# A selective scan that takes two channel tiles in one instruction

## The chip, the cores and the metric

The kernel runs on one core of a Trainium2 chip. The metric is the device time of one execution in microseconds, taken as the median of several runs. The core has a matrix engine (TensorE, PE in the profile; PEld is its weight load), VectorE (DVE), ScalarE (ACT), GpSimd (POOL) and SyncE (SP), which here issues nearly all DMA transfers. Each engine works through its own instructions in order.

## The reference, cut to what matters

One decoder layer in float32 on x of shape (8, 512, 512): a Mamba block, cross-attention with 16 heads, and a mixture of 32 experts with a shared expert, each followed by a residual sum and a layer norm. The change touches the Mamba block:

```python
xz = layernorm(x) @ in_proj_w                    # (b, s, 2048): x_main, z
x_main = silu(causal_conv(x_main, 4 taps))       # 1024 channels
dt, B, C = split(x_main @ x_proj_w)              # 32, 16, 16 wide
dt = softplus(dt @ dt_proj_w + dt_proj_b)        # (b, s, 1024)
h[t] = exp(A * dt[t]) * h[t-1] + dt[t] * B[t] * x_main[t]   # 1024 channels x 16 states
y[t] = sum over states of h[t] * C[t]
out = ((y + x_main * D) * silu(z)) @ out_proj_w + x
```

It also moves two buffers of the experts' routing: softmax over 32 experts, the best 4 of 8 groups, the best 4 experts, and their slots.

## The kernel before, in words

The program has three parts in sequence: `layers` (Mamba, attention, routing and shared expert of all 8 batches), `experts` (the 32 experts) and `finish` (last layer norm). The change is in `layers`.

*Tiles of the scan.* Channels lie on partitions: 1024 channels are 8 tiles of 128, taken as four pairs `q`. Time is cut into two chunks of 256 steps a batch, so there are 16 chunks. The 16 states are taken in groups of four. For one channel tile and one group the kernel keeps a state tile `h` of 128 partitions x 4 rows x 257 columns. Column 0 of each row holds the state carried from the chunk before; the other 256 hold dt·B·x, and after the scan the states. The partitions hold two halves of 64 channels with different states, which is why dt and dt·x are first copied by DMA into tiles `both` in that arrangement.

*One step.* A step is one (pair q, group g, tile ci of the pair); a chunk has 32, numbered k. Each step runs these functions:

- `carry` (L443, ScalarE) takes a state tile `h` from a ring of four and writes column 0 from `l_state`, or zeros from `l_nothing` in a batch's first chunk.
- `decays` (L437, ScalarE) writes exp(A·dt) of the *next* step into one of two tiles `l_da`, four activations of 256.
- `scan` (VectorE) writes the product dt·x·B into `h` (L449), runs the recurrence over all 4 x 257 columns in one scan instruction (L453; column 0 of `l_da` is zero, so rows do not mix), and in the first chunk of a batch stores the last column in `l_state` (L455).
- `collect` multiplies `h` by C (L470, VectorE) and sums over states on PE into the PSUM tile `py` (L474; at the first group also the D·x term, L462).

At the end of a pair `gated` multiplies `py` into the gate `zs` (L486).

*What else is in a chunk.* `prepare` (L392 on PE, then L402 to L418 on ScalarE and VectorE, then the DMA copies into `both`, L426) makes the next pair's dt and dt·x with softplus written as relu and logarithm. `bcast` (L381) copies rows of B and C to all partitions, tiles `bc`. Around fixed steps k stand the output projection of the chunk before (`back`, L503), the gate projection (`gate_x`, L305), and for the next chunk the layer norm, the input projection (L305), the convolution (`convolve`, VectorE taps at L339, buffer `xp`) and `x_proj` (L362). Between them the attention, the shared expert and the routing of the batch before are spread as "side" work by a running sum of costs: scores (L766), their row maxima on VectorE (`mx`, L768), exponentials (`eT`, L796), weighted sums (L808), dense products (L703), and the routing chain (`choose`, L546 to L602; `locate` after it).

*Order.* `do` holds back the later parts of a piece of work to the next call (`settle`), and the scheduler that builds the program fixes each engine's final order, so instructions of neighbouring steps are mixed. Pools with a fixed number of buffers decide how far a step can run ahead: `h` has four, `bc` four, `l_da` two, `both` two, and `u`, `dt`, `l`, `dtx`, `xp` one each.

Of the kernel before, what the change touches and what calls it, by code (L numbers as in the profile page):

```python
# [16 lines left out]
P = 128  # L17
B, S, D = 8, 512, 512
# [4 lines left out]
DI = 1024  # L23
NST = 16
RANK = 32
# [56 lines left out]
def layers(ctx, tc, a, x1d, filld, based, xbuf):  # L82
# [76 lines left out]
    nothing = cp.tile([P, NG, 1], F32, name="l_nothing")  # L159
    nc.gpsimd.memset(nothing, 0.0)  # L160
    das = [cp.tile([P, NG, T + 1], F32, name=f"l_da{i}") for i in range(2)]
    for da in das:
        nc.gpsimd.memset(da[:, :, 0:1], 0.0)

# [23 lines left out]
        channel_multiplier=0,  # L188
    )

    early = cp.tile([P, SC, E], F32, name="l_early")
    nc.gpsimd.iota(
        early, pattern=[[0, SC], [-1, E]], base=E, channel_multiplier=0, allow_small_or_imprecise_dtypes=True
    )
    first = cp.tile([P, SC, E], F32, name="l_first")
    nc.gpsimd.iota(
        first, pattern=[[0, SC], [CAP, E]], base=-SLOTS, channel_multiplier=0, allow_small_or_imprecise_dtypes=True
    )

    taken = cp.tile([P, SC + 1, E], F32, name="l_taken")  # L200
    nc.gpsimd.memset(taken, 0.0)
# [67 lines left out]

    piece = pieces()  # L270

    def load_x(b, t, f):
        f["xt"] = xt = p1.tile([P, NT_, D], F32, tag="xt", name="xt")
        nc.sync.dma_start(xt, a["x"][b, t * T : (t + 1) * T, :].rearrange("(j p) d -> p j d", p=P))
# [39 lines left out]
    def convolve(t, q, f):  # L314

        c0 = 2 * q
        ps = project(f, "ps_x")

        def first_tap():
            xp = p1.tile([P, 2, T + 3], F32, tag="xp", name="xp")  # L320
            if t == 0:
                nc.gpsimd.memset(xp[:, :, 0:3], 0.0)
            else:
                nc.gpsimd.tensor_copy(xp[:, :, 0:3], conv_tail[:, c0 : c0 + 2, :])
            nc.scalar.copy(xp[:, :, 3:], ps)
            if t < S // T - 1:
                nc.gpsimd.tensor_copy(conv_tail[:, c0 : c0 + 2, :], xp[:, :, T : T + 3])
            f["xs"][q] = xs = p2.tile([P, 2, T], F32, tag="xs", name="xs", bufs=6)
# [13 lines left out]

            return other_taps

        return first_tap
# [28 lines left out]
    def bcast(f, g):  # L374

        got = []
        for r0 in (g * NG, NST + g * NG):
            t = bcp.tile([P, NG // 2, T], F32, tag="bc", name="bc")
            for r in range(2):
                n0 = r0 + r * NG // 2  # L380
                nc.sync.dma_start(  # L381
                    t[r * HP : (r + 1) * HP], f["scr"][n0 : n0 + NG // 2, :].partition_broadcast(HP)
                )
            got.append(t.unsqueeze(1).to_broadcast([P, 2, NG // 2, T]))
        return got

    def prepare(q, f):

        ps = psm.tile([P, 2, T], F32, tag="mm", name="ps_dt")
        for i in range(2):  # L390
            c = 2 * q + i
            nc.tensor.matmul(  # L392
                ps[:, i, :], w_dt[:, c * P : (c + 1) * P], f["xd"][0:RANK, :], start=True, stop=True
            )

        def exponentials():
            u = p1.tile([P, 2, T], F32, tag="u", name="u")
            dt = p1.tile([P, 2, T], F32, tag="dt", name="dt")

            for i in range(2):  # L400
                c = 2 * q + i
                nc.scalar.activation(u[:, i, :], ps[:, i, :], AF.Abs, bias=b_dt[:, c : c + 1])  # L402
                nc.scalar.activation(dt[:, i, :], ps[:, i, :], AF.Relu, bias=b_dt[:, c : c + 1])
            nc.scalar.activation(u, u, AF.Exp, scale=-1.0)
            l = p1.tile([P, 2, T], F32, tag="l", name="l")
            nc.scalar.activation(l, u, AF.Ln, bias=1.0)
            w = dtx = p1.tile([P, 2, T], F32, tag="dtx", name="dtx")
            nc.scalar.activation(w, u, AF.Identity, bias=1.0)

            def both():  # L410

                nc.vector.scalar_tensor_tensor(w, w, -1.0, u, ALU.add, ALU.subtract)
                nc.vector.tensor_tensor(l, l, w, ALU.subtract)
# [19 lines left out]
    def decays(c, g, dt, da):  # L433

        for n in range(NG):
            j, m = n // 2, n % 2
            nc.scalar.activation(da[:, n, 1:], dt[:, c % 2, j, :], AF.Exp, scale=aneg[:, c, j, g, m : m + 1])  # L437

    def carry(t, c, g):

        last = state[:, c, g].unsqueeze(2)
        h = p3.tile([P, NG, T + 1], F32, tag="h", name="h", bufs=4)
        nc.scalar.copy(h[:, :, 0:1], last if t else nothing)  # L443
        return h

    def scan(t, c, g, dtx, bc, da, h):

        steps = h.rearrange("p (j m) t -> p j m t", j=2)[:, :, :, 1:]
        nc.vector.tensor_tensor(  # L449
            steps, dtx[:, c % 2].unsqueeze(2).to_broadcast([P, 2, NG // 2, T]), bc[0], ALU.mult  # L450
        )
        flat = h.rearrange("p n t -> p (n t)")
        nc.vector.tensor_tensor_scan(flat, da.rearrange("p n t -> p (n t)"), flat, 0.0, ALU.mult, ALU.add)  # L453
        if t < S // T - 1:
            nc.vector.tensor_copy(state[:, c, g].unsqueeze(2), h[:, :, T : T + 1])  # L455

    def collect(c, g, h, bc, py, f):


        if g == 0:  # L460
            for j in range(2):
# [8 lines left out]
        nc.vector.tensor_tensor(steps, steps, bc[1], ALU.mult)  # L470
        for m in range(NG // 2):
            for j in range(2):
                s = (g, m, c % 2)
# [70 lines left out]
    def choose(b, x2t, pl, st):  # L544
# [16 lines left out]
        eq = gm.tile(square, F32, tag="g_eq", name="g_eq")  # L561
        nc.vector.tensor_tensor(eq, other, own, ALU.is_equal)
        nc.vector.tensor_tensor(eq, eq, lower.unsqueeze(1).to_broadcast(square), ALU.mult)
        gt = gm.tile(square, F32, tag="g_gt", name="g_gt")
# [458 lines left out]
    for i, (b, t) in enumerate(chunks):  # L1023
# [8 lines left out]
        for k, (q, g, ci) in enumerate(steps):  # L1032
            if ci == 0:
                if (q, g) != (CC // 2 - 1, NST // NG - 1):
                    bcn = bcast(f, (g + 1) % (NST // NG))
                else:
                    bcn = bcast(nf, 0) if after else None
            h = carry(t, 2 * q + ci, g)

            if k + 1 < len(steps) or after:  # L1040
                nq, ng, ni = steps[(k + 1) % len(steps)]
                decays(2 * nq + ni, ng, (f if k + 1 < len(steps) else nf)["ready", nq][0], das[(n + 1) % 2])
            scan(t, 2 * q + ci, g, f["ready", q][1], bc, das[n % 2], h)
            n += 1
            if k % 8 == 0:
                if k:
                    gated(q - 1, f, py)
# [371 lines left out]
```

## Time and profile before

| | |
|---|---|
| median of 3 runs | 5617.29 us (5615.69 to 5618.11) |
| the profiled execution | 5620.06 us, its span 5617.3 us |
| busy PE / PEld / DVE / ACT / POOL | 4888.6 / 2725.6 / 4351.5 / 2592.2 / 546.1 us |
| scan L453: count, mean | 512, 2295 ns |
| product with B, L449 | 512, 1216 ns |
| product with C, L470 | 512, 1220 ns |
| exponentials L437 | 2048, 499 ns |
| scan stage, first scan to last | 84 to 3730 us of the span |

A row of the groups of instructions reads: line, engine, operation, output from inputs, shapes, count, then busy time and the mean of one in ns, then the idle time of the engine just before these instructions and what ended it. A row of the waits reads: who waited at which line for whom, the time in all, how often, the longest. A row of the timeline reads: start and duration in us, engine, line, operation, with the idle time before it in brackets.

### The profile page before, as it was taken

The numbers are of one execution on the slowest core, as the hardware profiler recorded it, in microseconds if no ns is written. First come the engines' busy times: TensorE is split into PE (matmuls) and PEld (weight loads), VectorE is DVE, ScalarE is ACT, GpSimd is POOL, SyncE is SP. The second block draws the span as 40 slices with busy tenths as digits, with TensorE's granted clock in tenths as the row PEclk, the third lists the DMA queues.
The fourth block names the chain that finished last, engine by engine and source line by source line (L and its number), as shares of the span: only waits on it lengthen the run. The fifth ranks groups of instructions, "written<-read, shape, count | busy, mean of one in ns | idle before, by whom it ended". The sixth has DMA issues, their size and how long they took to land. (4 is left out here: it accounts for less than half of the span.)

```text
span 5617.3 us, 60406 instructions
## 1 busy us (share of the span) xinstructions
PE 4888.6 (87%) x19752; PEld 2725.6 (49%) x19752; DVE 4351.5 (77%) x5738; ACT 2592.2 (46%) x5480; POOL 546.1 (10%) x424
## 2 busy tenths in 40 slices
PE   5667888888888988888888898879899999999994
PEld 3333344434433434443443443333577777777773
DVE  5988888989889998898989899854555655555554
ACT  4454555655556555565545656523122222222223
POOL 0000002001100200200010020010111111111111
PEclk8778999999999999999999999989899999999997
DMA  6777345434534534543463453431444444444444
GB/s 207 215 219 201 99 129 177 128 112 130 189 107 113 190 107 122 177 132 106 124 204 94 125 183 110 115 118 45 137 124 126 124 124 119 125 126 124 120 117 138
DMA packets 560426, 769.83 MB, mean 137 GB/s; under 512 B 135754, under 2 KB 268394, under 8 KB 560112
## 3 DMA queue, kind: packets, MB, share of 16 engines
q1 hardware_dynamic: 522608, 680.70, 40.2%
q0 software_dynamic: 33280, 76.90, 7.0%
q10 hardware_dynamic: 4224, 8.39, 0.4%
q8 instruction: 156, 2.56, 0.2%
q14 instruction: 158, 1.29, 0.1%
HBM read 508.68 MB, written 165.05 MB: 120 GB/s over the span
## 5 line engine op out<-in xcount | busy, mean ns | idle before, releaser
L437 ACT ACTIVATE l_da<-both,l_aneg 128x256 f32<-128x256 f32 x2048 | 888.4, 499 | 801.8 <-DVE h L453 759.7
L453 DVE TENSOR_TENSOR_SCAN h<-l_da,h 128x1028 f32<-128x1028 f32 x512 | 1171.2, 2295 | 48.5 <-ACT h L443 26.4
L474 PE MATMUL py<-h,l_twice 128*64 128x256 f32 x4096 | 628.1, 420 | 217.4 <-DVE h L470 217.3
L449 DVE TENSOR_TENSOR h<-both,bc 128x1024 f32<-128x1024 f32 x512 | 619.2, 1216 | 97.2 <-PE py L474 45.4
L470 DVE TENSOR_TENSOR h<-h,bc 128x1024 f32<-128x1024 f32 x512 | 623.5, 1220 | 6.0
L474 PEld LDWEIGHTS py<-h,l_twice 128*64 128x64 f32 x4096 | 295.3, 147 | 587.6 <-DVE h L470 260.7
L766 PE MATMUL ps_s<-l_ka,l_qa 64*128 64x512 f32 x1024 | 317.1, 699 | 142.9 <-DVE mx L768 142.7
L1199 PE MATMUL ps_h<-xT,w 128*128 128x320 f32 x1536 | 435.6, 433 | 0.0
L1279 POOL DMA_INDIRECT based<-y,xe x160 | 250.5, 1565 | 1317.2 <-ACT y L1302 579.9
L768 DVE TENSOR_REDUCE mx<-ps_s 128x2 f32<-128x1024 f32 x256 | 310.8, 1217 | 83.7 <-PE ps_s L766 82.9
L1220 DVE TENSOR_TENSOR hT<-ps_h,p 128x320 f32<-128x320 f32 x128 | 62.9, 492 | 374.7 <-PE ps_h L1199 374.6
L1199 PEld LDWEIGHTS ps_h<-xT,w 128*128 128x128 f32 x1536 | 292.4, 191 | 118.4 <-issue 0.8
L792 PE MATMUL ps_t<-l_qa,l_ka 64*128 64x512 f32 x1024 | 302.0, 654 | 15.8 <-ACT eT L796 11.9
L796 ACT ACTIVATE eT<-ps_t 128x1024 f32<-128x1024 f32 x256 | 259.1, 1013 | 111.9 <-PE ps_t L792 111.5
L808 PE MATMUL po<-eT,l_va 128*64 128x512 f32 x1024 | 279.2, 623 | 23.0 <-ACT raw L820 19.0
L1199 PE MATMUL ps_h<-t,s 128*128 128x320 f32 x1024 | 286.1, 432 | 0.0
L641 POOL DMA_INDIRECT xbuf<-x2t,dest x128 | 216.7, 1693 | 622.1 <-DVE dest L635 583.7
L305 PE MATMUL ps_z<-xnT,wm 128*128 128x256 f32 x1024 | 246.3, 395 | 31.2 <-DMA wm<-in_in_proj_w 28.4
L503 PE MATMUL po<-wm,zs 128*128 128x512 f32 x512 | 246.7, 634 | 13.0 <-DMA wm<-in_out_proj_w 8.5
L703 PE MATMUL ps_p<-x2T,wa 128*128 128x512 f32 x512 | 244.7, 627 | 11.1 <-DVE hT L883 9.1
L305 PE MATMUL ps_x<-xnT,wm 128*128 128x256 f32 x1024 | 245.3, 393 | 1.4 <-ACT xnT L294 1.1
L305 PEld LDWEIGHTS ps_z<-xnT,wm 128*128 128x128 f32 x1024 | 196.2, 196 | 83.7 <-ACT l_da L437 27.1
(225 smaller groups left out, 7397.0 us busy)
## 6 DMA issues: line engine op xcount, KB each, us to landing
bc<-scr SPq DMA_DIRECT2D x1024, 128.0 KB
w<-in_w SPq DMA_DIRECT2D x96, 1024.0 KB
wm<-in_in_proj_w SPq DMA_DIRECT2D x128, 512.0 KB
xbuf<-zero SPq DMA_DIRECT2D x32, 1362.5 KB
xe<-xbuf SPq DMA_DIRECT2D x32, 1362.5 KB
both<-dt SPq DMA_DIRECT2D x256, 128.0 KB
both<-dtx SPq DMA_DIRECT2D x256, 128.0 KB
wm<-in_out_proj_w SPq DMA_DIRECT2D x64, 512.0 KB
```

The costliest lines, as they stand in the source:

```text
L305: nc.tensor.matmul(ps[:, i, :], w[:, dc, i * P : (i + 1) * P], f["xnT"][:, dc, :], start=(dc == 0), stop=(dc == DC - 1),)
L437: nc.scalar.activation(da[:, n, 1:], dt[:, c % 2, j, :], AF.Exp, scale=aneg[:, c, j, g, m : m + 1])
L449: nc.vector.tensor_tensor(steps, dtx[:, c % 2].unsqueeze(2).to_broadcast([P, 2, NG // 2, T]), bc[0], ALU.mult)
L453: nc.vector.tensor_tensor_scan(flat, da.rearrange("p n t -> p (n t)"), flat, 0.0, ALU.mult, ALU.add)
L470: nc.vector.tensor_tensor(steps, steps, bc[1], ALU.mult)
L474: nc.tensor.matmul(py[j * HP : (j + 1) * HP, c % 2, :], twice, h[:, j * 2 + m, 1:], start=False, stop=(s == (NST // NG - 1, NG // 2 - 1, 1)),)
L766: nc.tensor.matmul(ps[:, j, :], qa[r, lt * P : (lt + 1) * P], ka[r, :], start=True, stop=True)
L768: return lambda: nc.vector.tensor_reduce(mx[:, lt, :].unsqueeze(2), ps, AX.X, ALU.max) and None
L792: nc.tensor.matmul(ps[:, j, :], ka[r, kc * P : (kc + 1) * P], qa[r, :], start=True, stop=True)
L796: nc.scalar.activation(eT, ps, AF.Exp)
L808: nc.tensor.matmul(po[j * 2 * HD : (j + 1) * 2 * HD, :], va[:, kc, i, j * HD : (j + 2) * HD], eT[:, j, :], start=(kc == 0), stop=(kc == SC ...
L1199: nc.tensor.matmul(ps, w[:, n, r * P : (r + 1) * P], x[:, n, :], start=not more and n == 0, stop=n == 1, skip_group_check=more,)
```

## The change

- `scan`, `carry` and `decays` work on both channel tiles of a pair at once: `h` and `l_da` have eight rows of 257 in place of four, the ring of `h` has three such tiles. They run at the first half step (`ci == 0`) of each pair; `collect` still runs for each tile on its half of `h`. The exponentials are written one pair step ahead, `k + 2`.
- The dt product of the next pair is issued at k = 0, 8, 16, and for the next chunk at 26, in place of 3, 11, 19, 27.
- dt's weights are no constant tile any more but are loaded by pairs, one load ahead, in two buffers.
- Buffers: `l` shares the buffer of `xp`; `xs` has five buffers for six; the routing's `early` and `first` hold one row and are read by broadcast; its `g_eq` and `g_gt` lie in a buffer of the shared tag `row`.

The diff, cut to its core:

```diff
-    w_dt = const("w_dt", [RANK, DI], a["dt_proj_w"])
...
-    das = [cp.tile([P, NG, T + 1], F32, name=f"l_da{i}") for i in range(2)]
+    das = [cp.tile([P, 2 * NG, T + 1], F32, name=f"l_da{i}") for i in range(2)]
...
+    def dts():
+        got = None
+        for n in range(B * (S // T) * CC // 2 + 1):
+            q = n % (CC // 2)
+            nxt = p2.tile([RANK, 2 * P], F32, tag="wdt", name="wdt")
+            nc.sync.dma_start(nxt, a["dt_proj_w"][:, 2 * q * P : 2 * (q + 1) * P])
+            if got is not None:
+                yield got
+            got = nxt
...
-            l = p1.tile([P, 2, T], F32, tag="l", name="l")
+            l = p1.tile([P, 2, T + 3], F32, tag="xp", name="l")[:, :, 0:T]
...
-    def carry(t, c, g):
-        last = state[:, c, g].unsqueeze(2)
-        h = p3.tile([P, NG, T + 1], F32, tag="h", name="h", bufs=4)
-        nc.scalar.copy(h[:, :, 0:1], last if t else nothing)
+    def carry(t, q, g):
+        h = p3.tile([P, 2 * NG, T + 1], F32, tag="h", name="h", bufs=3)
+        nc.scalar.copy(h.rearrange("p (i n) t -> p i n t", i=2)[:, :, :, 0], last(q, g) if t else none)
...
+        both = [P, 4, NG // 2, T]
         nc.vector.tensor_tensor(
-            steps, dtx[:, c % 2].unsqueeze(2).to_broadcast([P, 2, NG // 2, T]), bc[0], ALU.mult
+            steps,
+            dtx.rearrange("p i j t -> p (i j) t").unsqueeze(2).to_broadcast(both),
+            bc[0].to_broadcast(both),
+            ALU.mult,
         )
...
         if t < S // T - 1:
-            nc.vector.tensor_copy(state[:, c, g].unsqueeze(2), h[:, :, T : T + 1])
+            nc.vector.tensor_copy(last(q, g), h.rearrange("p (i n) t -> p i n t", i=2)[:, :, :, T])
...
+        h = h[:, c % 2 * NG : (c % 2 + 1) * NG]
...
-            h = carry(t, 2 * q + ci, g)
-
-            if k + 1 < len(steps) or after:
-                nq, ng, ni = steps[(k + 1) % len(steps)]
-                decays(2 * nq + ni, ng, (f if k + 1 < len(steps) else nf)["ready", nq][0], das[(n + 1) % 2])
-            scan(t, 2 * q + ci, g, f["ready", q][1], bc, das[n % 2], h)
-            n += 1
+            if ci == 0:
+                h = carry(t, q, g)
+
+                if k + 2 < len(steps) or after:
+                    nq, ng, _ = steps[(k + 2) % len(steps)]
+                    decays(nq, ng, (f if k + 2 < len(steps) else nf)["ready", nq][0], das[(n + 1) % 2])
+                scan(t, q, g, f["ready", q][1], bc, das[n % 2], h)
+                n += 1
...
-            if k % 8 == 3:
-                if q + 1 < CC // 2:
-                    do(prepare, q + 1, f)
-                elif after:
-                    do(prepare, 0, nf)
+            if k in (0, 8, 16):
+                do(prepare, q + 1, f)
+            if k == 26 and after:
+                do(prepare, 0, nf)
```

More of the change, by code (lines that the diff above doesn't have):

```diff
@@ L158, in layers @@
     state = cp.tile([P, CC, NST // NG, NG], F32, name="l_state")
-    nothing = cp.tile([P, NG, 1], F32, name="l_nothing")
-    nc.gpsimd.memset(nothing, 0.0)
-    das = [cp.tile([P, NG, T + 1], F32, name=f"l_da{i}") for i in range(2)]
+    none = cp.tile([P, 2, NG], F32, name="l_none")
+    nc.gpsimd.memset(none, 0.0)
+    das = [cp.tile([P, 2 * NG, T + 1], F32, name=f"l_da{i}") for i in range(2)]
     for da in das:
@@ L189, in layers @@
     )
[L191 to L198, printed above, removed]
+    early = cp.tile([P, E], F32, name="l_early")
+    nc.gpsimd.iota(early, pattern=[[-1, E]], base=E, channel_multiplier=0, allow_small_or_imprecise_dtypes=True)
+    early = early.unsqueeze(1).to_broadcast([P, SC, E])
+    first = cp.tile([P, E], F32, name="l_first")
+    nc.gpsimd.iota(first, pattern=[[CAP, E]], base=-SLOTS, channel_multiplier=0, allow_small_or_imprecise_dtypes=True)
+    first = first.unsqueeze(1).to_broadcast([P, SC, E])
     taken = cp.tile([P, SC + 1, E], F32, name="l_taken")
@@ L270, in layers @@
     piece = pieces()
+    def dts():
[7 more added lines that the diff above has]
+            got = nxt
+    w_dt = dts()
     def load_x(b, t, f):
@@ L327, in first_tap @@
                 nc.gpsimd.tensor_copy(conv_tail[:, c0 : c0 + 2, :], xp[:, :, T : T + 3])
-            f["xs"][q] = xs = p2.tile([P, 2, T], F32, tag="xs", name="xs", bufs=6)
+            f["xs"][q] = xs = p2.tile([P, 2, T], F32, tag="xs", name="xs", bufs=5)
             for i in range(2):
@@ L383, in bcast @@
                 )
-            got.append(t.unsqueeze(1).to_broadcast([P, 2, NG // 2, T]))
+            got.append(t.unsqueeze(1))
         return got
     def prepare(q, f):
+        w = next(w_dt)
         ps = psm.tile([P, 2, T], F32, tag="mm", name="ps_dt")
         for i in range(2):
-            c = 2 * q + i
             nc.tensor.matmul(
-                ps[:, i, :], w_dt[:, c * P : (c + 1) * P], f["xd"][0:RANK, :], start=True, stop=True
+                ps[:, i, :], w[:, i * P : (i + 1) * P], f["xd"][0:RANK, :], start=True, stop=True
             )
@@ L431, in prepare, with decays, last, scan @@
         return exponentials
[L433 to L437, printed above, removed]
-    def carry(t, c, g):
-        last = state[:, c, g].unsqueeze(2)
-        h = p3.tile([P, NG, T + 1], F32, tag="h", name="h", bufs=4)
-        nc.scalar.copy(h[:, :, 0:1], last if t else nothing)
-        return h
-    def scan(t, c, g, dtx, bc, da, h):
-        steps = h.rearrange("p (j m) t -> p j m t", j=2)[:, :, :, 1:]
+    def decays(q, g, dt, da):
+        for i in range(2):
+            for n in range(NG):
+                j, m = n // 2, n % 2
+                nc.scalar.activation(
+                    da[:, i * NG + n, 1:], dt[:, i, j, :], AF.Exp, scale=aneg[:, 2 * q + i, j, g, m : m + 1]
+                )
+    def carry(t, q, g):
+        h = p3.tile([P, 2 * NG, T + 1], F32, tag="h", name="h", bufs=3)
+        nc.scalar.copy(h.rearrange("p (i n) t -> p i n t", i=2)[:, :, :, 0], last(q, g) if t else none)
+        return h
+    def last(q, g):
+        return state[:, 2 * q : 2 * q + 2, g]
+    def scan(t, q, g, dtx, bc, da, h):
+        steps = h.rearrange("p (j m) t -> p j m t", m=NG // 2)[:, :, :, 1:]
+        both = [P, 4, NG // 2, T]
         nc.vector.tensor_tensor(
-            steps, dtx[:, c % 2].unsqueeze(2).to_broadcast([P, 2, NG // 2, T]), bc[0], ALU.mult
+            steps,
+            dtx.rearrange("p i j t -> p (i j) t").unsqueeze(2).to_broadcast(both),
+            bc[0].to_broadcast(both),
+            ALU.mult,
         )
@@ L468, in collect @@
                 )
+        h = h[:, c % 2 * NG : (c % 2 + 1) * NG]
         steps = h.rearrange("p (j m) t -> p j m t", j=2)[:, :, :, 1:]
-        nc.vector.tensor_tensor(steps, steps, bc[1], ALU.mult)
+        nc.vector.tensor_tensor(steps, steps, bc[1].to_broadcast([P, 2, NG // 2, T]), ALU.mult)
         for m in range(NG // 2):
@@ L560, in choose @@
         own = gs.unsqueeze(3).to_broadcast(square)
-        eq = gm.tile(square, F32, tag="g_eq", name="g_eq")
+        both = p3.tile([P, D], F32, tag="row", name="g_eq").rearrange("p (n j g h) -> p n j g h", n=2, j=SC, g=G)
+        eq, gt = both[:, 0], both[:, 1]
         nc.vector.tensor_tensor(eq, other, own, ALU.is_equal)
         nc.vector.tensor_tensor(eq, eq, lower.unsqueeze(1).to_broadcast(square), ALU.mult)
-        gt = gm.tile(square, F32, tag="g_gt", name="g_gt")
         nc.vector.tensor_tensor(gt, other, own, ALU.is_gt)
```

## The prediction

> **What bounds the kernel now.** I read the page's busy shares first, then a window over the scan stage (84 to 3730 us, from the first scan to the last), then who waits for whom inside it, then single rows for prices. In the window answer the columns are busy time and instruction count of PE, PEld, DVE, ACT, POOL, then granted clock, DMA share and GB/s.
>
> ```profile
> PE 4888.6 (87%) x19752; PEld 2725.6 (49%) x19752; DVE 4351.5 (77%) x5738; ACT 2592.2 (46%) x5480; POOL 546.1 (10%) x424
> ...
> 84.00:3730.00 3646.00, 3098.48 (x12635) 1482.10 (x12636) 3304.17 (x3768) 2041.92 (x4353) 252.52 (x190) 0.92 0.49 144
> ```
>
> Over the whole span PE looks like the bound (87%). Inside the scan stage it is VectorE: 3304.17 of 3646 us (90.6%), PE 85%, ScalarE 56%. The waits say the same.
>
> ```profile
> PE py L474 <- DVE h L470: 217.3, 69, 15.1
> PE ps_s L766 <- DVE mx L768: 141.9, 80, 4.4
> PE ps_m L775 <- DVE mx L768: 44.6, 39, 3.4
> ...
> DVE h L449 <- PE py L474: 45.4, 27, 3.7
> DVE zs L486 <- PE py L474: 41.1, 20, 4.3
> DVE h L453 <- ACT h L443: 26.4, 16, 2.0
> ```
>
> PE stands 404 us behind VectorE; VectorE stands only some 45 us for a free state tile (L449) and 26 us for the carried column (L453, whose copy itself waits for that tile). So VectorE's work sets the pace, and most of its 342 us of idle time are short waits spread over sixteen chunks.
>
> **The prices.** What merging can save is the part of an instruction that does not grow with its size.
>
> ```profile
> L453 DVE TENSOR_TENSOR_SCAN h<-l_da,h 128x1028 f32<-128x1028 f32 x512 | 1171.2, 2295 | 48.5 <-ACT h L443 26.4 <-ACT l_da L437 6.4
> L449 DVE TENSOR_TENSOR h<-both,bc 128x1024 f32<-128x1024 f32 x512 | 619.2, 1216 | 97.2 <-PE py L474 45.4 <-DMA both<-dtx 26.8 <-DMA bc<-scr 11.2
> L413 DVE TENSOR_TENSOR l<-l,dtx 128x512 f32<-128x512 f32 x64 | 44.1, 688 | 1.0
> L455 DVE COPY l_state<-h 128x4 f32<-128x4 f32 x256 | 42.1, 166 | 2.9
> ```
>
> A TENSOR_TENSOR of 512 takes 688 ns, of 1024 takes 1216: the fixed part is 2 x 688 - 1216 = 160 ns. The 4-element copy (166 ns) is almost nothing else. No second size of the scan is in the trace; its fixed part lies between 0 and 2295 - 1028 x 2 x 1.031 = 175 ns (two passes at the TENSOR_TENSOR's slope of 528 ns per 512); I take 160, by the copy and the product beside it.
>
> But these are durations, and the timeline shows that they are not the pitch:
>
> ```profile
> 2306.44 1.22 DVE L449 TENSOR_TENSOR h<-both,bc 128x1024 f32<-128x1024 f32 x1
> 2307.57 0.29 DVE L585 TENSOR_TENSOR g_oh<-g_oh,l_early 128x128 f32<-128x128 f32 x1
> ...
> 2232.28 1.21 DVE L449 TENSOR_TENSOR h<-both,bc 128x1024 f32<-128x1024 f32 x1
> 2233.40 1.22 DVE L470 TENSOR_TENSOR h<-h,bc 128x1024 f32<-128x1024 f32 x1
> 2234.53 2.30 DVE L453 TENSOR_TENSOR_SCAN h<-l_da,h 128x1028 f32<-128x1028 f32 x1
> ```
>
> An instruction that does not need the one before it starts 0.09 us before that one's end (2306.44 + 1.22 = 2307.66 against 2307.57; the same twice in the second group). One that needs it starts later: across the stage the scan follows its own product by 0.10 us, the others by 0.03 to 0.04. So a removed instruction is worth 160 - 90 = 70 ns, and a removed dependent neighbour a further 0.19 us (product to scan) or 0.12 us (the rest).
>
> **The change, part by part.**
>
> Scan by pairs. Products L449 go from 512 to 256, scans L453 from 512 to 256, state copies L455 from 256 to 128; the 512 products with C (L470) stay. 640 instructions x 0.07 = 45 us. In the order in which the built programs' instructions stand on VectorE, dependent neighbours fall from 164 product-scan and 262 others to 85 and 119: 79 x 0.19 + 143 x 0.12 = 32 us. All of this lies on the bounding engine: **77 us**. By whole durations it would be 512 x 0.160 + 128 x 0.166 = 103 us, the upper bound; the lower, with a scan that has no fixed part, is 77 - 256 x 0.07 = 59.
>
> A rule weighed against this: the Trainium skill's Perfetto Trace Analysis (Optimizing Scalar/DVE Operations) gives about 60 ns of overhead for a VectorE operation on SBUF and says that the profiled latency shows about twice that; by its figure the first term would be an estimated 640 x 60 ns = 38 us instead of 45. The same section warns that where VectorE is not saturated but makes other engines wait, smaller instructions may finish sooner; at 90.6% with PE waiting on it this stage lies between the two cases, and by that rule alone the gain would be doubtful.
>
> Three tiles of pairs in place of four of single tiles. A product now waits for the pair three back, so five to six half steps of room instead of four. That loosens the 45.4 us (L449 after py). Bounds 0 to 72 us (both rows above, 45.4 + 26.4); I take 25, since a pair tile comes free only when both its halves have gone through PE.
>
> ScalarE. 256 carry copies fewer (x 0.193 us = 49) and, in the built order, 87 table loads instead of 135 (48 x 1.283 = 62): 111 us less of an engine idle for 1604 us of this stage. On the path: 0, a gain of some tens of us at most. The exponentials into da become eight in a row (8 x 0.43 = 3.4 us of pitch, from four taking 1.71) behind the scan two back. They are hidden by one pair scan (2 x 2.295 - 0.16 = 4.4 us) and the products around it, at least 9 us. If that cover failed, the scan would wait, and so would what stands behind them on ScalarE: the exponentials eT and the copies raw, for which PE waits only 3.6 and 19 us now.
>
> The boundary of two batches. In the built order of the changed kernel the routing chain (L546 to L602, 46 small instructions) and the next chunk's first softplus stand together after the last scan of the chunk, with no scans among them; before, scans were mixed in. After the chain's one ScalarE step comes, on ScalarE: four table loads 5.1, SiLU of xs 2.5 and of hT 1.9, three copies 1.7, then xd 0.4 and the softplus activations 3.8, with x_proj and the dt product on PE between (about 2.4): near 18 us. VectorE's cover is some 43 instructions at 0.3 us, 13 us. So about 4 us idle at each of 7 boundaries: **-28 us**; bounds 0 to -70. After the softplus, its copies to `both` land some 3 us later and the first eight exponentials take 3.4; two slot products, the rest of the routing and two scan products (4.5 us) cover that.
>
> dt product at steps 0, 8, 16, 26. 64 products of two matmuls, as before, moved past the gate projection (L305); each dt is now needed one half step earlier (exponentials for k = 8 at k = 6, not 7) and issued three earlier (for the next chunk one), so no wait is added. Its DMA copies on SP (L426) move with it. Price 0; if late, decays would stand as they do now for `both<-dt` (38.1 us in all, 22 times).
>
> dt's weights by pairs. 65 loads of 32 KB through SP for one of 128 KB. Each is issued a whole pair of tiles, about 3646 / 64 = 57 us, ahead. SP's issue rows take 0.3 to 0.7 us, so 0 on the path, and at most 64 x 0.6 = 38 if every issue delayed the `bc` copies queued behind it.
>
> The rest: `l` shares the buffer of `xp`, so the logarithm (L406) can wait for the convolution's taps (L339, six of 0.48 us) with da's exponentials queued behind it: 0 to 16 x 2.9 = 46 us, taken as 0 since the built order places the softplus after the taps and ScalarE has slack. Routing constants read by broadcast and `g_eq`, `g_gt` in a shared row: same instruction counts and sizes, 0, with 0 to 2 us a batch for a row still being written out.
>
> Sum: 77 + 25 - 28 = 74 us. The profiled execution took 5620.06 us (span 5617.3); 5620 - 74 = 5546, and the median of the three runs lies 2.8 below the profiled one. I say **5545**.
>
> **The rivals.**
>
> *Longer blocks starve PE (slower).* Place: L470 and L768 behind one scan of 4.4 us instead of 2.3. PE now waits 188 times for these two (69 + 80 + 39). If each wait grew by the added 2.14 us that is 402 us; it decides from 77/402, a fifth of them. With a third, 134 - 77 = 57 slower: 5675. For it: the waits are already 404 us. Against it: the same scan time in half as many blocks is met half as often, and PE has 547 us of idle time in the stage to absorb some.
>
> *The gain is given back at boundaries (no change).* If the batch boundary costs 10 us instead of 4, and the wider buffers bring nothing: 77 - 70 = 7 us: 5610.
>
> *More than forecast.* Full room from the three tiles (72), no boundary loss: 77 + 72 = 149: 5470.
>
> **How the numbers follow.** Forecast (5500 to 5605) 0.60; more than that 0.15; no change 0.07; slower 0.18. A measurement of this kernel tells some 0.2%, 11 us, from no change. Faster 0.75, same 0.07, slower 0.18. The range leaves out the far ends of the first and last case: 5485 to 5640.
>
> **What would show it.** Right: in the scan stage VectorE's busy time falls by some 75 to 100 us, scans read near 4.43 us and the wide product near 2.27, the stage (first to last scan) shrinks from 3646 to near 3572, and VectorE's idle share stays near 9%; L449's wait for py shrinks; at each batch boundary a VectorE wait of a few us for ScalarE's dtx appears. Wrong: a scan over 4.6 us; PE's waits for L470 or L768 up by over 100 us; VectorE's busy share of the stage below 88%; or scans waiting for da.

## The result: 2.5% slower, and the profile after

The changed kernel took 5758.12 us (median of four runs, 5755.88 to 5760.15) against 5617.70 for the kernel before, a ratio of 1.025 [1.0232, 1.0267]: 140 us slower. The forecast was 5545 us, with a range of 5485 to 5640. Its profiled execution took 5756.47 us (span 5754.1).

In the changed kernel the scan is L472, the product with B L465, the product with C L490, the sum over states L494, the convolution's taps L349, the row maxima L788, the logits L559 and the first routing step L566. The page after, busy times and then two groups of instructions:

```profile
PE 4895.2 (85%) x19752; PEld 2732.2 (47%) x19752; DVE 4293.2 (75%) x5098; ACT 2489.5 (43%) x5176; POOL 572.4 (10%) x424
...
L472 DVE TENSOR_TENSOR_SCAN h<-l_da,h 128x2056 f32<-128x2056 f32 x256 | 1135.1, 4437 | 23.0 <-ACT h L455 16.1
...
L465 DVE TENSOR_TENSOR h<-both,bc 128x2048 f32<-128x2048 f32 x256 | 585.0, 2287 | 163.8 <-PE py L494 92.0
```

The single instructions did what they were expected to. The pair scan takes 4437 ns (two single ones took 4590), the wide product 2287 (two took 2432), and VectorE's busy time in the program falls from 4351.5 to 4293.2 us. Yet the stage from the first scan to the last grew, as the windows over it show, first before, then after (columns as in the prediction):

```profile
84.00:3722.00 3638.00, 3094.19 (x12620) 1479.61 (x12620) 3297.42 (x3751) 2041.92 (x4353) 252.52 (x190) 0.92 0.49 144
84.00:3826.00 3742.00, 3060.94 (x12499) 1466.89 (x12500) 3222.07 (x3071) 1929.79 (x4038) 279.50 (x191) 0.91 0.48 140
```

The last scan starts at 3826 us, before at 3722. VectorE's busy time in the stage is 3222 us (3297 before), but its idle time went from 340 to 520 us, and PE's from 544 to 681. PE's busy time in the stage is 33 us shorter: that work comes after the last scan, where the first product of the experts now starts 319 us behind it instead of 285. So 104 us were lost in the scan stage and 34 behind it: 138 of the 140.

Who waits for whom after the change, from 84 to 3870 us (who, for whom, total us, times, longest). The window ends 44 us behind the start of the last scan, so it holds the seventh of the eight routings, which came ahead of the last scan before:

```profile
PE py L494 <- DVE h L490: 201.5, 57, 12.2
...
PE ps_s L786 <- DVE mx L788: 109.8, 61, 6.8
...
DVE h L465 <- PE py L494: 92.0, 39, 5.6
...
DVE g_m L566 <- PE ps_l L559: 67.3, 7, 11.1
PE ps_m L795 <- DVE mx L788: 66.9, 23, 6.6
...
PE ps_p L723 <- DVE attT L861: 47.1, 6, 7.9
DVE xs L349 <- ACT xs L341: 46.9, 21, 5.2
DVE mx L788 <- PE ps_s L786: 46.4, 27, 3.9
...
DVE h L465 <- DMA bc<-scr: 42.5, 17, 9.0
DVE hT L903 <- PE ps_p L723: 42.3, 21, 3.3
...
DVE dtx L422 <- ACT dtx L418: 40.1, 13, 3.7
...
DVE h L465 <- DMA both<-dtx: 28.4, 17, 4.0
...
DVE k L708 <- PE ps_p L723: 25.0, 6, 4.8
...
DVE zs L506 <- PE py L494: 17.9, 10, 3.9
```

PE's three waits for VectorE that the prediction showed (217, 142, 45) are 202, 110 and 67: together 26 us *less*. What grew are VectorE's own waits: for a free state tile 45 to 92, for the logits (L566) from 0.4 to 67, for scores (L788) 13 to 46, for `bc` 2 to 43, for the dense products (L903 with L708) 3 to 67, for dtx 27 to 40, for the convolution's inputs (L349) 33 to 47. PE's waits in other rows grew too, for the attention's result `attT` from 8 to 47 and for the output projection's weights from 0 to 36. Some fell: VectorE's for the gate's input `py` (L506) from 41 to 18, for the next chunk's x from 36 to 0. No one row holds the loss.

How such a wait arises can be followed at a batch boundary. First VectorE's timeline before (start, duration), at the layer norm in front of the routing. Its steps on 128x4 elements (L54 to L77) each need the one before, or ScalarE between:

```profile
2262.52 0.16 DVE L54 TENSOR_SCALAR v<-mv 128x4 f32<-128x4 f32 x1
2262.59 2.29 DVE L453 TENSOR_TENSOR_SCAN h<-l_da,h 128x1028 f32<-128x1028 f32 x1
...
2266.65 0.16 DVE L77 SCALAR_TENSOR_TENSOR less<-mv,o 128x4 f32<-128x4 f32 x1
2271.15 0.69 DVE L486 TENSOR_TENSOR zs<-zs,py 128x512 f32<-128x512 f32 x1 [4.34 <-PE py L474]
...
2280.34 2.30 DVE L453 TENSOR_TENSOR_SCAN h<-l_da,h 128x1028 f32<-128x1028 f32 x1 [0.63 <-ACT l_da L437]
...
2286.19 0.28 DVE L546 TENSOR_REDUCE g_m<-ps_l 128x4 f32<-128x128 f32 x1
```

One scan and one product with C lie within the chain, which ends 4.3 us after its start. Routing starts 19.4 us behind its end (L546) and does not wait for the logits; VectorE has scans and products up to there, with 4.34 us of waiting for the gate's input and 0.63 for `l_da`. The same place after:

```profile
2344.93 0.17 DVE L54 TENSOR_SCALAR v<-mv 128x4 f32<-128x4 f32 x1
...
2347.34 0.17 DVE L60 TENSOR_TENSOR m<-m,r 128x4 f32<-128x4 f32 x1
2347.41 4.44 DVE L472 TENSOR_TENSOR_SCAN h<-l_da,h 128x2056 f32<-128x2056 f32 x1
2351.76 0.15 DVE L61 TENSOR_SCALAR m<-m 128x4 f32<-128x4 f32 x1
2351.81 2.29 DVE L465 TENSOR_TENSOR h<-both,bc 128x2048 f32<-128x2048 f32 x1
...
2355.22 0.16 DVE L77 SCALAR_TENSOR_TENSOR less<-mv,o 128x4 f32<-128x4 f32 x1
...
2356.43 4.44 DVE L472 TENSOR_TENSOR_SCAN h<-l_da,h 128x2056 f32<-128x2056 f32 x1
2360.91 2.36 DVE L490 TENSOR_TENSOR h<-h,bc 128x1024 f32<-128x1024 f32 x2
2374.09 0.29 DVE L566 TENSOR_REDUCE g_m<-ps_l 128x4 f32<-128x128 f32 x1 [10.82 <-PE ps_l L559]
```

The scheduler set one large instruction behind nearly every small step, and one is 4.44 us long, one 2.29 and three 1.2: the chain takes 10.5 us. The logits are there 18.7 us after its end (2355.38 to 2374.09), and before the routing also started 19.4 us behind it; but of the scans and products that stand ahead of the routing only 7.9 us are left behind the chain. They end at 2363.27, and VectorE stands still for 10.82 us, 5.9 more than the two waits before. Six of the boundaries are like this one, with waits of 10.6 to 11.1 us for the logits; at the seventh, behind the last scan, it is 2.4.

### The profile page after: what moved, and what is told of

It reads as the page before. It is cut to its first block, busy times and chain, and to the rows that moved or that the text cites. A ratio compares the mean times of both kernels' runs of the same rounds, so it can differ in the third digit from the quotient of the medians.

```text
span 5754.1 us, 59366 instructions
## 1 busy us (share of the span) xinstructions
PE 4895.2 (85%) x19752; PEld 2732.2 (47%) x19752; DVE 4293.2 (75%) x5098; ACT 2489.5 (43%) x5176; POOL 572.4 (10%) x424
## 5 line engine op out<-in xcount | busy, mean ns | idle before, releaser
L448 ACT ACTIVATE l_da<-both,l_aneg 128x256 f32<-128x256 f32 x2048 | 872.1, 500 | 724.0 <-DVE h L472 612.5
L472 DVE TENSOR_TENSOR_SCAN h<-l_da,h 128x2056 f32<-128x2056 f32 x256 | 1135.1, 4437 | 23.0 <-ACT h L455 16.1
L494 PE MATMUL py<-h,l_twice 128*64 128x256 f32 x4096 | 633.1, 421 | 201.8 <-DVE h L490 201.5
L465 DVE TENSOR_TENSOR h<-both,bc 128x2048 f32<-128x2048 f32 x256 | 585.0, 2287 | 163.8 <-PE py L494 92.0
L490 DVE TENSOR_TENSOR h<-h,bc 128x1024 f32<-128x1024 f32 x512 | 613.9, 1220 | 3.1 <-DMA bc<-scr 0.3
L494 PEld LDWEIGHTS py<-h,l_twice 128*64 128x64 f32 x4096 | 310.3, 149 | 544.3 <-DVE h L490 244.1
L788 DVE TENSOR_REDUCE mx<-ps_s 128x2 f32<-128x1024 f32 x256 | 310.8, 1220 | 115.9 <-PE ps_s L786 114.9
L523 PE MATMUL po<-wm,zs 128*128 128x512 f32 x512 | 262.5, 663 | 68.1 <-DMA wm<-in_out_proj_w 44.1
L828 PE MATMUL po<-eT,l_va 128*64 128x512 f32 x1024 | 292.8, 647 | 24.0 <-ACT eT L816 19.7
L661 POOL DMA_INDIRECT xbuf<-x2t,dest x128 | 239.5, 1871 | 584.3 <-DVE dest L655 545.9
L315 PE MATMUL ps_x<-xnT,wm 128*128 128x256 f32 x1024 | 246.1, 393 | 11.4 <-DMA wm<-in_in_proj_w 11.1
L1219 PEld LDWEIGHTS ps_h<-t,s 128*128 128x128 f32 x1024 | 194.6, 190 | 81.1
```

The costliest lines, as they stand in the source:

```text
L315: nc.tensor.matmul(ps[:, i, :], w[:, dc, i * P : (i + 1) * P], f["xnT"][:, dc, :], start=(dc == 0), stop=(dc == DC - 1),)
L448: nc.scalar.activation(da[:, i * NG + n, 1:], dt[:, i, j, :], AF.Exp, scale=aneg[:, 2 * q + i, j, g, m : m + 1])
L465: nc.vector.tensor_tensor(steps, dtx.rearrange("p i j t -> p (i j) t").unsqueeze(2).to_broadcast(both), bc[0].to_broadcast(both), ALU.mult,)
L490: nc.vector.tensor_tensor(steps, steps, bc[1].to_broadcast([P, 2, NG // 2, T]), ALU.mult)
L494: nc.tensor.matmul(py[j * HP : (j + 1) * HP, c % 2, :], twice, h[:, j * 2 + m, 1:], start=False, stop=(s == (NST // NG - 1, NG // 2 - 1, 1)),)
L523: nc.tensor.matmul(pos[j], yg[:, c, j * P : (j + 1) * P], w[:, i, :], start=(c == 0), stop=(c == CC - 1))
```

## The experiments

Each kernel's ratio is to the kernel before, on the same chip. In the expectations, theory A lays the loss to the earlier dt product, B to the merged instructions, C to the changed buffers and the room that they give, D to the shared buffer of `l` and `xp` or the fifth of `xs`; E lays it to handing work over by pairs, whatever the length of the instructions, and so keeps the loss where attention is left out; F says that the room for scans and the place of the dt product must fit each other.

### Undoing or adding one part at a time

**e1_single_dt_early**: the kernel before with dt at the new steps.

```diff
-            if k % 8 == 3:  ...
+            if k in (0, 8, 16):
+                do(prepare, q + 1, f)
+            if k == 26 and after:
+                do(prepare, 0, nf)
```

> The kernel before with one edit: the dt product of the next pair at k = 0, 8, 16, 26 in place of 3, 11, 19, 27; scans stay single, all buffers as before. Theory A (dt issued early lets the scans run ahead, so that they end before the chunk's other work and VectorE stands idle at the boundary of two batches): slower than before, by 60 to 140 us of the change's 140, with VectorE waiting about 11 us for the routing logits ps_l at each of 7 batch boundaries, as in the changed kernel. Theory B (longer scan blocks starve PE): no more than 15 us from the kernel before. Theory C (three tiles of pairs let the scans run ahead): no more than 15 us from the kernel before.

5651.91 us, 1.0072 [1.0055, 1.0089]. The moved dt, priced at 0 in the prediction, costs 38 us without any pair, less than A's 60 to 140. The wait for the logits is only 2 us here, so that is not how.

**e2_pair_dt_late**: the changed kernel with dt back at `k % 8 == 3`.

```diff
-            if k in (0, 8, 16):
-                do(prepare, q + 1, f)
-            if k == 26 and after:
-                do(prepare, 0, nf)
+            if k % 8 == 3:  ...
```

> The changed kernel with the dt product back at k = 3, 11, 19, 27; pairs, three tiles, shared buffers and dt's weights by pairs stay. Theory A: faster than the kernel before by 40 to 90 us (5530 to 5580), since the 77 us of merged instructions remain and the waits at the boundary go. Theory B and theory C: within 30 us of the changed kernel (5730 to 5790).

5808.56 us, 1.0353 [1.0336, 1.037]: worse than the changed kernel and above what every theory had here. With pairs the early dt is needed. VectorE's waits for the taps' inputs are 88, for dtx 84 and for `both` 77 us. A falls as the cause of the whole.

**e3_pair_last_dt_late**: the changed kernel with only the last pair's dt later.

```diff
-            if k in (0, 8, 16):
+            if k in (0, 8, 19):
```

> The changed kernel with only the dt product of the last pair back at its place: k = 0, 8, 19, 26. Theory A in its narrow form (only the last pair's dt decides whether scans end before the chunk's other work): most of the change's loss goes, 5560 to 5640, and the 11 us waits for ps_l are gone. Theory A in its wide form (each early dt costs): about a quarter of the loss goes, 5700 to 5740. Theory B and C: as the changed kernel, 5730 to 5790.

5716.88 us, 1.0179 [1.0162, 1.0196]. 41 us come back, as A's wide form had it, and the wait for the logits falls from 67 to 20.

**e4_pair_two_tiles**: the changed kernel with two pair tiles, and with `l` and `xs` in their old buffers.

```diff
-        h = p3.tile([P, 2 * NG, T + 1], F32, tag="h", name="h", bufs=3)
+        h = p3.tile([P, 2 * NG, T + 1], F32, tag="h", name="h", bufs=2)
```

> The changed kernel with two state tiles of pairs in place of three (the room of the kernel before, four single tiles), and with l and xs in buffers of their own again. Theory C (room to run ahead does the harm): at least 70 us faster than the changed kernel. Theory A: within 30 us of the changed kernel, or slower, since products then wait for the tile two back; the wait for ps_l stays. A theory D, that the shared buffer of l and xp or the fifth xs buffer does the harm, expects here the same as theory C, and is told from it by run e2, where the sharing stays.

5813.03 us, 1.0358 [1.034, 1.0375]. About 1% worse than three tiles, where C and D had it at least 70 us better; D falls for good with e6, which keeps those buffers. (The edits of `l` and `xs` are not shown.) The wait for a state tile is 119 us with two, 92 with three.

**e5_pair_scan_split** and **e6_pair_both_split**: the changed kernel with all its tiles, buffers and steps, but with the scan of the pair, and then its product as well, written as two instructions one after the other.

```diff
-        flat = h.rearrange("p n t -> p (n t)")
-        nc.vector.tensor_tensor_scan(flat, da.rearrange("p n t -> p (n t)"), flat, 0.0, ALU.mult, ALU.add)
+        for i in range(2):
+            one = slice(i * NG, (i + 1) * NG)
+            flat = h[:, one].rearrange("p n t -> p (n t)")
+            nc.vector.tensor_tensor_scan(flat, da[:, one].rearrange("p n t -> p (n t)"), flat, 0.0, ALU.mult, ALU.add)
```

> The changed kernel with the scan of a pair issued as two scans of 128x1028, one for each channel tile; the product of the pair, the tiles, the exponentials and the dt places stay as changed. Theory B (the 4.4 us scan as one block keeps PE and ScalarE waiting): most of the loss that early dt alone does not explain goes, 5640 to 5700. Theory E (what costs is that work is handed over by pairs: the eight exponentials, the state tile and da come free or ready only as a pair): it stays, 5750 to 5810, a little above the changed kernel since 256 scans come back at 0.07 to 0.19 us each (18 to 49 us).

For e6 also:

```diff
-            dtx.rearrange("p i j t -> p (i j) t").unsqueeze(2).to_broadcast(both),
...
+        for i in range(2):
+            steps = h[:, i * NG : (i + 1) * NG].rearrange("p (j m) t -> p j m t", j=2)[:, :, :, 1:]
...
+                steps, dtx[:, i].unsqueeze(2).to_broadcast(both), bc[0].to_broadcast(both), ALU.mult
```

> As the run before, and the product of the pair split in two as well, so that no instruction is longer than in the kernel before; pairs remain only in the tiles, the carry and state copies, the eight exponentials and the place of the scans in the steps. Theory B: near the single kernel with dt early (5652), 5640 to 5690. Theory E: 5770 to 5850.

5690.89 us, 1.0122 [1.0106, 1.0139], and 5660.73 us, 1.0072 [1.0055, 1.0089]. B holds. The four ratios make a ladder: dt early +0.7%; pair tiles, three of them, shared buffers and weights by pairs +0.0% in all (e6 is where e1 is); product merged +0.5%; scan merged on top of it +1.3%. Some 97 of the 140 us come with the merging itself. The page of e6 gives the instructions' side of it, the window the stage's, the waits where the time had gone, and the timeline the same boundary:

```profile
L472 DVE TENSOR_TENSOR_SCAN h<-l_da,h 128x1028 f32<-128x1028 f32 x512 | 1154.9, 2284 | 9.4 <-ACT h L455 8.9
...
L466 DVE TENSOR_TENSOR h<-both,bc 128x1024 f32<-128x1024 f32 x512 | 610.8, 1217 | 142.3 <-PE py L494 97.5
```

```profile
84.00:3740.00 3656.00, 3077.20 (x12544) 1478.77 (x12545) 3244.08 (x3584) 1962.60 (x4065) 312.79 (x191) 0.91 0.50 144
```

```profile
DVE h L466 <- PE py L494: 97.5, 56, 3.8
...
DVE dtx L422 <- ACT dtx L418: 25.8, 9, 4.1
...
DVE xs L349 <- ACT xs L341: 24.3, 14, 2.7
...
DVE hT L903 <- PE ps_p L723: 19.5, 12, 2.7
...
DVE h L466 <- DMA both<-dtx: 6.8, 7, 1.7
...
DVE g_m L566 <- PE ps_l L559: 0.2, 1, 0.2
```

```profile
2289.77 0.14 DVE L54 TENSOR_SCALAR v<-mv 128x4 f32<-128x4 f32 x1
...
2297.44 0.15 DVE L77 SCALAR_TENSOR_TENSOR less<-mv,o 128x4 f32<-128x4 f32 x1
...
2319.92 0.28 DVE L566 TENSOR_REDUCE g_m<-ps_l 128x4 f32<-128x128 f32 x1
```

Splitting costs VectorE 22 us of busy time in the stage (3244 against 3222) and takes 108 off its idle time (412 against 520). Within the stage, up to its last scan, 65 of that are at the logits, 22 to 23 each at the taps and `both`, 14 to 15 each at the dense products (L903) and dtx; other waits grew, that for the routing's exponential (L570) most, from 2 to 16. The wait for a state tile stays (98 against 92): it does not come with the merging. At the boundary the layer norm's chain takes 7.8 us here (from 2289.77), still longer than before; but 22.3 us of other work stand between it and the routing, and nothing waits up to there. The same place in e1, where nothing is merged:

```profile
2290.48 0.15 DVE L54 TENSOR_SCALAR v<-mv 128x4 f32<-128x4 f32 x1
...
2299.25 0.13 DVE L77 SCALAR_TENSOR_TENSOR less<-mv,o 128x4 f32<-128x4 f32 x1
...
2320.65 0.28 DVE L546 TENSOR_REDUCE g_m<-ps_l 128x4 f32<-128x128 f32 x1
```

The chain takes 8.9 us, with 21.3 us of work behind it. So most of the chain's growth, from 4.3 us, came with the early dt, and merging adds 2.6 (7.82 to 10.45). The wait for the logits comes from what is left to do behind the chain: 7.9 us in the changed kernel, over 21 in e1 and e6. Whether the length of the instructions or the order built around them leaves so little is not shown.

### The other half of the merge, and room

**e7_single_scan_wide_product**: the kernel before with the product with B written for both channel tiles in pair tiles, scans single, dt late.

```diff
-            scan(t, 2 * q + ci, g, f["ready", q][1], bc, das[n % 2], h)
+            if ci == 0:
+                h = carry(t, q, g)
+                inputs(h, f["ready", q][1], bc)
...
+            scan(t, q, g, ci, das[n % 2], h)
```

> The kernel before with only the product dt x B made for a pair at once, in three tiles of pairs; scans, exponentials, da and the dt places stay single as before, the state and carry copies are by pairs. Theory B: 256 products and 128 copies fewer, 384 x 0.07 to 0.19 us = 27 to 73 us less of VectorE's time and blocks of at most 2.3 us: 5560 to 5600. Theory E: the state tile is handed over by pairs but da and the exponentials are not; if the state tile is what costs, 5680 or more; if the exponentials are, 5560 to 5620.

5773.42 us, 1.0279 [1.0254, 1.0304], 170 us above B's forecast and in line with E's (5680 or more if the state tile is what costs), though E had missed e5 and e6. Something besides the length of instructions was at work, and the waits pointed to the dt product: `both` 113, the taps' inputs 105, dtx 68 us. e8 asks whether more room alone does that.

**e8_single_six_tiles**: the kernel before with six single state tiles in place of four.

```diff
-        h = p3.tile([P, NG, T + 1], F32, tag="h", name="h", bufs=4)
+        h = p3.tile([P, NG, T + 1], F32, tag="h", name="h", bufs=6)
```

> The kernel before with six state tiles in place of four and nothing else. It measures what room alone brings: the 45 us for which the product waits for a free tile could go. Theory C (room to run ahead does harm): slower by over 20 us. Otherwise 5575 to 5620.

5778.17 us, 1.0278 [1.0261, 1.0295]: two more buffers, and 2.8% slower, as C had it. The waits:

```profile
DVE dtx L412 <- ACT dtx L408: 106.8, 28, 6.8
...
DVE xs L339 <- ACT xs L331: 100.3, 32, 5.2
...
DVE h L449 <- DMA both<-dtx: 83.0, 25, 8.0
...
DVE h L449 <- PE py L474: 5.0, 7, 1.5
```

The wait for a state tile is gone (45 to 5), as room should make it. But the first three rows, which F lays to scans that run ahead to where the next pair's dt is not made yet, were 27, 33 and 27 us with four tiles. **e9_six_tiles_dt_early** adds e1's edit to it.

> Six single state tiles (as e8) and the dt product at k = 0, 8, 16, 26 (as e1), all else as before. Theory F (with more room the scans reach the next pair's dt before it is made, and VectorE then waits for softplus and its copies; early dt takes that away): well below e8, 5640 to 5700. Theory C (room itself does the harm): e8's 165 us and e1's 38 add up, 5780 to 5830.

5656.96 us, 1.0068 [1.0051, 1.0085], 121 us better than e8:

```profile
DVE h L449 <- PE py L474: 51.6, 38, 3.0
...
DVE xs L339 <- ACT xs L331: 33.2, 29, 2.2
...
DVE dtx L412 <- ACT dtx L408: 30.8, 15, 5.0
...
DVE h L449 <- DMA both<-dtx: 6.9, 2, 3.7
```

F holds, and C's sum of both losses (5780 to 5830) does not. Early dt costs 0.7% with four tiles and gains 2.1% with six. This fits the change's moving of dt, and e2 and e7, which keep the late dt with three pair tiles and are worse than the change itself; e7 with early dt was not run.

**e10_single_last_dt_late**: e1 with the last pair's dt back at 19 and the next chunk's at 27. **e15_six_tiles_last_dt_late**: e9 with 19 in place of 16.

```diff
-            if k in (0, 8, 16):
+            if k in (0, 8, 19):
...
-            if k == 26 and after:
+            if k == 27 and after:
```

(The second of the two pairs of lines is in e10 alone.)

> The kernel before with the dt product at k = 0, 8, 19, 26: as e1, but the last pair's dt is back at its place. Narrow form of theory A (the last pair's early dt lets the scans of a chunk end before its other work): e1's loss of 38 us goes, 5600 to 5630. Wide form (each early dt costs its share): 5635 to 5650.

> Six single tiles with dt at k = 0, 8, 19, 26: e9 with the last pair's dt back. If the last pair's dt alone sets the loss at the end of a chunk, 5600 to 5630, and a candidate for a version faster than both; if room and dt place must fit for every pair, the last pair meets e8's waits and it is 5680 or more.

e10: 5614.22 us, 0.9988 [0.9978, 0.9997]; e15: 5687.31 us, 1.0112 [1.0092, 1.0132]. With four tiles e1's loss came from the places at 16 and 26, and is gone; with six, the later place of the last pair loses 0.4%. e10 is the only kernel with the whole layer that is not above the kernel before, and 0.1% is less than the 0.2% that this measurement tells.

**e14_split_last_dt_late**: e6 with e3's edit, 19 in place of 16, to be held against e3.

> The kernel of e6 with the last pair's dt back at k = 19, so e3 with product and scan issued singly. If merging costs by the length of the instructions, it costs here what it cost between e6 and the changed kernel, some 97 us: 5600 to 5640. If its cost came only with the early dt of the last pair, e14 is near e3: 5690 to 5730.

5635.35 us, 1.0026 [1.0014, 1.0039]. With this dt place too the merging costs 1.5% (e3: 1.0179). In both of these the chain of the layer norm takes 1.7 us, so that chain is an example of the loss and not its whole; here the difference stands at a free state tile (72 in e14, 124 in e3), at the gate (32 and 62) and at `both` (46 and 67), while e14 waits longer for the output projection (62 and 7).

### Is it the mixed work that makes merging dear?

**e11_light_before**, **e12_light_after** and **e13_light_split** are the kernel before, the changed one and e6, each without attention's scores, maxima, exponentials and weighted sums (the queries stand in for the attention's result).

```diff
-        add(0, spread, 0)
-        add(0, spread, 1)
+        add(0, lambda: st.__setitem__("attT", st["qT"]))
...
-        for n in range(pairs * SC + 4):
+        for n in range(0):
```

> The kernel before without the attention's scores, maxima, exponentials and weighted sums (the queries take the place of the attention's output), so that PE has much idle time and VectorE no row maxima. It is the base for the next run. Expected 5617 less about 375 us of VectorE's work: 5100 to 5350 in both theories.

> The changed kernel without the same part of the attention. Theory B (long blocks cost because PE, ScalarE and VectorE wait for one another when all are busy): with PE light the merging pays as forecast, 20 to 80 us faster than e11. Theory E (hand-over by pairs costs by itself): still slower than e11 by over 40 us.

> The kernel of e6 (pairs in tiles and copies, scan and product issued singly, dt early) without the attention's scores, maxima, exponentials and weighted sums, as e11 and e12. Against e12 it shows what merging product and scan does when PE is light; with the attention it cost 97 us (5661 to 5758). Theory B (the longer instructions cost through waits of engines that are all near full): merging pays here, e13 is 5 to 40 us above e12, 4833 to 4868. If merging costs by itself (a slower scan, a later hand-over to PE), e13 is at least 20 us below e12.

4833.44, 4827.46 and 4817.44 us; to the kernel before, 0.8597 [0.8583, 0.8612], 0.8588 [0.8574, 0.8603] and 0.8569 [0.8555, 0.8584]. All three are far below the 5100 to 5350 forecast for e11. The loss is gone, but no gain takes its place: the change is 6 us from the kernel before, and merged and split are 10 us apart with intervals that overlap, to the wrong side for merging. Neither theory's numbers for e12 and e13 were met. The windows over the scan stage, e12 and then e13:

```profile
84.00:3057.00 2973.00, 2397.94 (x9730) 1261.36 (x9731) 2872.51 (x2832) 1644.77 (x3667) 484.18 (x192) 0.90 0.58 167
```

```profile
84.00:3053.00 2969.00, 2429.35 (x9740) 1265.26 (x9741) 2893.70 (x3344) 1666.42 (x3673) 414.37 (x192) 0.89 0.58 167
```

VectorE is busy 97% of either stage. Merging takes 21 us off its busy time (2872.5 against 2893.7) and adds 25 to its idle time (100 against 75). Even here what it saves is not time.

## Why the prediction was wrong

*VectorE bounds the stage; 77 us for 640 instructions.* This is the step that failed first. Both single prices were good (scan 4437 ns against 4.43 us, product 2287 against 2.27), and the stage's busy time fell by the foreseen 75 us (17 of them by work that moved behind the last scan, as the program's fell by 58), but busy time was read as time. What the runs showed in its place: from e6 to the change, merging takes 18 us off VectorE's busy time in the program and makes the kernel 97 us slower. Of the 58 us, 40 are already gone in e6, where nothing but the state copies is merged (the product and the scan are still 512 each); so merging 512 instructions into their neighbours took 36 ns each and not 70. The 32 us for fewer dependent neighbours show in part: in the traces, VectorE's gaps under 0.3 us in the stage fall from 44 to 30 us in all, but the longer ones rise from 297 to 490.

*The rival "longer blocks starve PE", dismissed because the same scan time in half as many blocks is met half as often.* Its sign was right and its dismissal was the wrong step. That argument holds for work that meets the scan by chance. The timelines show another case: large instructions stand behind most small steps of a chain, so the chain meets them step by step. That is a small part of the loss, though: 2.6 us at each of six boundaries between e6 and the change, and none in e3 and e14, where merging still costs 1.5%. The rival's own place was wrong too: PE's waits for L470 and L768 did not grow but fell by 26 us. What grew is VectorE waiting for other engines, at the boundary for work that follows its own small steps, and PE's waits in rows that the prediction did not price. The prediction's test "PE's waits up by over 100 us" would have missed it; "VectorE's busy share below 88%" caught it (86%).

*The rule of the Trainium skill* (Perfetto Trace Analysis, Optimizing Scalar/DVE Operations) that smaller instructions may finish sooner where VectorE is not saturated but makes others wait was shown beside the sum and not used. e6 against the changed kernel agrees with it (89% busy in e6, 97 us); e12 against e13 shows that at 97% busy little of that cost is left.

*+25 us for three pair tiles.* Wrong in sign: the wait for a tile doubled (45 to 92). e4 shows that two would be worse, e6 that it is there without the merging. Room is not the only thing in it: with late dt the wait is 23 us for three pair tiles (e2) and 5 for six single ones (e8), with early dt 92 and 52 (e9). A pair tile comes free only when PE has gone through both halves; this was said, but that it is the reason is not shown.

*Boundary -28 us, 4 us at each of 7.* Right as far as it went: the forecast wait for dtx stands at six boundaries with 3.66 us each. The wait for the logits, 10.6 to 11.1 us at the same six, was no part of it.

*The dt product at new steps, price 0.* Wrong: 38 us (e1), all of it from the places at 16 and 26 (e10). The step asked only whether a dt comes late. How an earlier one costs was not settled: e1's waits grew by 13 to 22 us in several rows (a state tile 45 to 60, the carry 26 to 41) and fell in others, with no one place.

*ScalarE off the path, table loads fewer, dt's weights by pairs, shared `l` 0.* Borne out: ScalarE's busy time fell by 103 us with no gain, and e6, which has all the buffers, stands where e1 does in all.

What stays open: each kernel gets an engine order of its own from the scheduler. The runs tell that merging costs 1.7% (5758 against 5661 us) in the order that it gets, and where the waits stand; they do not part the length of the instruction from the order built around it. An order held fixed by hand was not tried.

## What to carry to other kernels

On an engine that runs long independent work between short dependent steps for others, a long instruction delays the step behind it, and the engine waits at the chain's end if too little other work is left; before merging, look at what small chains pass through the engine and what stands behind them, not only at the fixed cost saved. Room to run ahead and the place where the next input is made are one choice: two more buffers alone cost 2.8%, moving the producer alone 0.7%, and both together 0.7%, so neither can be judged with the other held fixed. Price an engine's saving by the stage's busy and idle time together.

## What was not expected of the hardware

Merging two neighbouring instructions takes 131 to 147 ns off their durations (2 x 2284 - 4437 and 2 x 1217 - 2287, by the rows of e6 and after), yet from e6 to after the program's busy time fell by only 36 ns for each instruction removed. Independent neighbours on VectorE already overlap by 0.08 to 0.09 us (the prediction's rows, and 2299.72 + 2.27 = 2301.99 against a start at 2301.91 in e6), so most of the fixed part that a group row shows was hidden before.
